# Six neighbouring channels to a partition, and the first image's group statistics by two masked products

## The chip, the cores and the metric

The kernel runs on one core of a Trainium2 chip. The metric is the device time of one launch in microseconds (us); lower is better. Engines are named as in the profile: PE is TensorE (PEld its weight loads), DVE is VectorE, ACT is ScalarE, POOL is GpSimd, and SP is SyncE, which here only issues transfers.

## The reference

Two residual layers run in series over four images of 32 x 32 positions and 768 channels. Each layer normalises its input in 32 groups of 24 neighbouring channels, applies attention with 12 heads of width 64 and decomposed relative positions, projects, and adds the input back.

```python
def _gn(v, G=32, eps=1e-5):
    g = v.reshape(B_, H_, W_, G, C_ // G)
    m = jnp.mean(g, axis=(1, 2, 4), keepdims=True)
    s = jnp.var(g, axis=(1, 2, 4), keepdims=True)
    return ((g - m) / jnp.sqrt(s + eps)).reshape(v.shape)

def attention(x, ...):                      # layer 1 has biases and another position table
    q, k, v = heads(x @ Wqkv)
    bias = rel_h[..., :, None] + rel_w[..., None, :]
    attn = softmax(scale * (q @ k.T) + bias)
    return heads_back(attn @ v) @ Wproj + bproj

x = x + attention_0(_gn(x))
x = x + attention_1(_gn(x))
```

The mean and the variance of a group are taken over all 1024 positions and over its 24 channels.

## The kernel before

The input is held channels first: an image is 768 rows (channels) of 1024 positions, in fp32. A channel chunk `c` (six of them, `NC`) is 128 channels, one to a partition; half `h` of an image is 512 positions. So a tile `xn_0_c_h` is 128 x 512, and partition p of chunk c holds channel 128c + p. All weights are laid out on the host to match, before the timed span.

There are eight image passes (two layers of four images), each of six pairs of heads, each of eight units of 128 query positions. A loop over the 384 units writes out by hand the order of instructions on every engine. `load_x` brings tiles of x, `fetch` the residuals (`res`) and output weights, `put_result` adds a projected part and stores it (`part`, then `mid` between the layers, or `out`).

A unit computes scores (L443), softmax (L455, L459, L473 or L471), transposes the probabilities on DVE (L479), writes them to memory (`td`) and reads them back in another order (`pt`) for the product with v (L508). Beside that the query, key and value products of the next pair (L285, L313) and output projections run. The q, k products use sums and differences of weight quarters and of image tiles: `combine` on POOL makes weight quarters (L129), `sums` on POOL makes image sums s2, s3, s4 (L257).

All of this starts with a normalisation. `stats` takes bn_stats of each half tile (L188) and bn_aggr per channel (L191), which gives mean and variance per channel in `mv` (128 x 6 x 2). The group step, `norm`, has five stages: `gather` writes `mv` to memory as 768 pairs (`per`, L208), `by_group` reads it back with one group to a partition (`g`, 32 x 24 x 2, L211), `groups` combines means and variances (L215 to L218), `inverses` makes scale and shift per channel and writes them to memory (`back`, L225), and `spread` reads them with a channel to a partition (`nrm`, L228). `apply` then scales each tile in place, on ACT (L233) or on DVE (L235).

For image 0 all five stages stand one behind the other, on the ACT queue, before the first product. For the seven later image passes they are spread over the units of pair 3 of the pass before, on the SP queue, with the applies in pair 4:

```python
queue = nc.sync if im else nc.scalar
queue.dma_start(out=per.rearrange("(c p) s -> p c s", p=P), in_=mv_of[im])
...
stages, apply = norm(0)
for n in sorted(stages):
    stages[n]()
for stage in range(2):
    combine(0, stage)
for h in range(2):
    for c in range(NC):
        apply(c, h, c % 2 == 1)
```

The SP queue is one queue for `td`, `pt`, `rel`, `res`, `part`, weights and x, in the order in which the loop issues them. PSUM tiles of tag `m` (two buffers) and the `pt` tiles (two buffers) rotate.

Of the kernel before, what the change touches and what calls it, by code (L numbers as in the profile page):

```python
# [31 lines left out]
FP = mybir.dt.float32  # L32
AF = mybir.ActivationFunctionType
ALU = mybir.AluOpType
ENGINES = {getattr(mybir.EngineType, e) for e in ("PE", "DVE", "Activation", "Pool", "SP")}

P = 128
B, HW, C = 4, 32, 768
S = HW * HW
NH, D = 12, 64  # L40
NC = C // P
NT = S // P
NG, GS = 32, C // 32
EPS = 1e-5
SCALE = D ** -0.5
HALF = 512
LAYERS = 2
NP = NH // 2
# [8 lines left out]
def attention_blocks(ctx: ExitStack, tc: tile.TileContext, a: dict, out: bass.AP):  # L57
    nc = tc.nc
# [12 lines left out]
    ptpool = ctx.enter_context(tc.tile_pool(name="pt", bufs=2))  # L71
# [3 lines left out]
    small = ctx.enter_context(tc.tile_pool(name="small", bufs=4))  # L75
# [4 lines left out]
    ps_m = ctx.enter_context(tc.tile_pool(name="ps_m", bufs=2, space=PSUM))  # L80
# [3 lines left out]
    srcs = [[a["x"][b] for b in range(B)], mid]  # L84
    dsts = [mid, [out[b] for b in range(B)]]
# [4 lines left out]
    xn_of = {im: [[], []] for im in range(NI)}  # L90
    w_of, wv_of, wo_of = {}, {}, {}

    def load_x(im, c, h, half=None):

        l, b = images[im]
        if c == len(xn_of[im][h]):
            xn_of[im][h].append(xpool.tile([P, HALF], FP, tag="xn", name=f"xn_{im}_{c}_{h}"))
        half = h if half is None else half
        nc.sync.dma_start(
            out=xn_of[im][h][c],  # L100
            in_=srcs[l][b][c * P : (c + 1) * P, half * HALF : (half + 1) * HALF],
        )

    def weights_of(g, name):
# [32 lines left out]
    def combine_values(g):  # L137

        w = wv_of[g]
        nc.gpsimd.tensor_tensor(w[:, NB:], w[:, NB:], w[:, :NB], ALU.subtract)  # L140

    for c in range(NC):
        for h in range(2):
            load_x(0, c, h)
# [9 lines left out]
    for l in range(LAYERS):  # L154
        tab = const.tile([P, 2, 2 * HW], FP, tag=f"tab{l}", name=f"tab{l}")
        nc.gpsimd.memset(tab, 0.0)
        for i, ax in enumerate("hw"):
            src = a[f"rel{ax}{l}"]
            n = src.shape[1]
# [10 lines left out]
    for l in range(LAYERS):  # L170
# [7 lines left out]
    mv_of = {  # L178
        im: const.tile([P, NC, 2], FP, tag=f"mv{im}", name=f"mv_{im}") for im in range(NI)
    }  # L180
    half_stats = {}

    def stats(im, c, i, x):

        if im not in half_stats:
            half_stats[im] = small.tile([P, NC, 2, 6], FP, tag="st", bufs=2, name=f"st_{im}"), set()
        st, done = half_stats[im]
        nc.vector.bn_stats(st[:, c, i, :], x)  # L188
        done.add((c, i))
        if (c, 1 - i) in done:  # L190
            nc.vector.bn_aggr(mv_of[im][:, c, :], st[:, c].rearrange("p i s -> p (i s)"))  # L191

    def norm(im):

        per = dram2.tile([C, 2], FP, tag="per", name=f"per_{im}")
        back = dram2.tile([C, 2], FP, tag="back", name=f"back_{im}")  # L200
        g = small.tile([NG, 2, GS, 2], FP, tag="g", bufs=1, name=f"g_{im}")
        st = small.tile([NG, 2, 6], FP, tag="gst", bufs=1, name=f"gst_{im}")
        mv = small.tile([NG, 3, 2], FP, tag="gmv", bufs=1, name=f"gmv_{im}")
        nrm = small.tile([P, NC, 2], FP, tag="nrm", bufs=2, name=f"nrm_{im}")
        queue = nc.sync if im else nc.scalar

        def gather():
            queue.dma_start(out=per.rearrange("(c p) s -> p c s", p=P), in_=mv_of[im])  # L208

        def by_group():  # L210
            queue.dma_start(out=g[:, 0, :, :], in_=per.rearrange("(g k) s -> g k s", k=GS))  # L211

        def groups():
            for k in range(2):
                nc.vector.bn_stats(st[:, k, :], g[:, 0, :, k])  # L215
                nc.vector.bn_aggr(mv[:, k, :], st[:, k, :])
            nc.vector.tensor_scalar(mv[:, 2, 0:1], mv[:, 0, 1:2], mv[:, 1, 0:1], EPS, ALU.add, ALU.add)
            nc.scalar.activation(mv[:, 2, 1:2], mv[:, 2, 0:1], AF.Sqrt)  # L218

        def inverses():  # L220
            nc.vector.reciprocal(mv[:, 2, 0:1], mv[:, 2, 1:2])
            nc.vector.tensor_scalar(mv[:, 2, 1:2], mv[:, 0, 0:1], mv[:, 2, 0:1], -1.0, ALU.mult, ALU.mult)
            for k in range(2):
                nc.vector.tensor_copy(g[:, 1, :, k], mv[:, 2, k : k + 1].to_broadcast([NG, GS]))
            queue.dma_start(out=back.rearrange("(g k) s -> g k s", k=GS), in_=g[:, 1, :, :])  # L225

        def spread():
            queue.dma_start(out=nrm, in_=back.rearrange("(c p) s -> p c s", p=P))  # L228

        def apply(c, h, scalar=True):  # L230
            x = xn_of[im][h][c]
            if scalar:
                nc.scalar.activation(x, x, AF.Identity, bias=nrm[:, c, 1:2], scale=nrm[:, c, 0:1])  # L233
            else:
                nc.vector.tensor_scalar(  # L235
                    x, x, nrm[:, c, 0:1], nrm[:, c, 1:2], ALU.mult, ALU.add
                )

        return {1: gather, 2: by_group, 4: groups, 5: inverses, 7: spread}, apply

    sum_tiles = {}
# [279 lines left out]
    def cuts(im):  # L521
        return [0, NC // 2, NC] if im + 1 < NI else [0, NC // 2, NC - 1, NC]
# [6 lines left out]
    part_of, res_of, sum_of = {}, {}, {}  # L529
    fetched = [0, 0]  # L530

    def fetch(upto):

        while fetched[0] <= min(upto, len(parts) - 1):
            im, p, o, i = parts[fetched[0]]
            c0, c1 = cuts(im)[p : p + 2]
            if i == 0:
                w = wopool.tile([P, NC // 2, P], FP, tag="wo", name=f"wo_{im}_{p}_{o}")
                nc.sync.dma_start(
                    out=w[:, : c1 - c0, :],  # L540
                    in_=a[f"wo{images[im][0]}"][o][:, c0 * P : c1 * P].rearrange(
                        "p (c o) -> p c o", o=P
                    ),
                )
                for c in range(c0, c1):
                    wo_of[im, o, c] = w[:, c - c0, :]
            fetched[0] += 1
        while fetched[1] <= min(upto, len(parts) - 1):
            im, p, o, i = parts[fetched[1]]
            l, b = images[im]  # L550
            if (p, o, i) == (0, 0, 0) and im + 1 < NI:
                part_of[im] = dram2.tile([C, S], FP, tag="part", name=f"part_{im}")
            res = iopool.tile([P, HALF], FP, tag="res", name=f"res_{im}_{p}_{o}_{i}")
            res_of[im, p, o, i] = res
            src = srcs[l][b] if p == 0 else part_of[im]
            nc.sync.dma_start(out=res, in_=src[o * P : (o + 1) * P, i * HALF : (i + 1) * HALF])
            fetched[1] += 1

    def fetch_last():
# [36 lines left out]
    def put_result(im, p, o, i, t):  # L596
        l, b = images[im]
        end = im + 1 == NI
        rows = slice(o * P, (o + 1) * P)
        cols = slice(i * HALF, (i + 1) * HALF)  # L600
        if end and p == 0:
            sum_of[o, i] = xpool.tile([P, HALF], FP, tag="xn", name=f"sum_{o}_{i}")
        to = sum_of[o, i] if end else res_of[im, p, o, i]
        if p == 0:
            res = res_of[im, p, o, i]
            nc.vector.scalar_tensor_tensor(to, t, bo[l][:, o : o + 1], res, ALU.add, ALU.add)
        else:
            nc.vector.tensor_tensor(to, t, to, ALU.add)
        if p == 1 and l + 1 < LAYERS:
            stats(im + B, o, i, to)  # L610
        dst = (part_of[im] if p == 0 and not end else dsts[l][b])[rows, cols]
        if not end:
            early.append(lambda: nc.sync.dma_start(out=dst, in_=to))
        elif p == 2:
            nc.sync.dma_start(out=dst, in_=to)
        if i == 1 and (im, p, o, i) in place:
            if end:
                fetch(place[im, p, o, i] + 4)
            else:
                later.append(lambda: fetch(place[im, p, o, i] + 4))  # L620
# [63 lines left out]
    with tc.manual_schedule(engines=ENGINES):  # L684
        for c in range(NC):
            for i in range(2):
                stats(0, c, i, xn_of[0][i][c])
        stages, apply = norm(0)
        for n in sorted(stages):
            stages[n]()  # L690
        for stage in range(2):
            combine(0, stage)
        for h in range(2):
# [46 lines left out]
        for at, (g, n) in enumerate(units):  # L740
            im, pair = divmod(g, NP)
            end = im + 1 == NI
            if n == 0:
# [7 lines left out]
                if pair == 3 and not end:  # L751
                    stages, apply = norm(im + 1)
# [6 lines left out]
            if (pair, n) in loads and not end:  # L759
                load_x(im + 1, loads[pair, n], 0)  # L760
            if pair == 4 and n in (1, 2) and not end:
                for c in range(3 * n - 3, 3 * n):
                    load_x(im + 1, c, 1)
            if im + 1 < B:
                if pair == 0 and n < NC:
                    load_x(im + 1, n, 0, 1)
                c = n - 2 if pair == 0 else loads.get((pair, n - 2), loads.get((pair - 1, n + 6), -1))
# [44 lines left out]
            if n == 4 and pair % 2 and g + 1 < NPAIR:  # L812
                combine_values(g + 1)
# [76 lines left out]
```

## Time and profile before

| what | value |
|---|---|
| median of 3 runs | 3369.71 us (3365.89 to 3370.19) |
| the profiled execution: its time | 3373.25 us |
| the profiled execution: its span | 3370.8 us |
| PE busy | 3319.2 us, 98% |
| DVE, ACT, POOL busy | 2415.5, 2039.6, 2332.4 us |
| transfers | 1046.97 MB in 534777 packets, mean 311 GB/s |
| transfers under 512 B | 149728 packets |
| first product of image 0 | 26.72 us after the start of the span |

The span is what the profiler saw from the first to the last instruction; the execution's own time is 2.45 us longer. A busy PE is matmuls in flight, whose ends are modelled. Idle time of an engine counts only where it is on the chain that ended last.

### The profile page before, as it was taken

How to read it: one execution, taken by the hardware profiler on the slowest of the kernel's cores; microseconds unless marked ns; L12 is line 12 of the kernel's file. 1: busy time of each engine (PE TensorE's matmuls, PEld its weight loads, DVE VectorE, ACT ScalarE, POOL GpSimd, SP SyncE). 2: the span in 40 equal slices, each digit the busy share in tenths (PEclk: the TensorE clock that was granted, in tenths of full speed). 3: DMA queues.
4: the chain of work that ended last, by engine and by line, in shares of the span. 5: the costliest groups of instructions: out<-in, count | busy, mean ns of one | idle time of the engine just before them, and what ended most of it. 6: DMA issues, size and time to landing. Idle time of an engine off the chain costs nothing.

```text
span 3370.8 us, 58086 instructions
## 1 busy us (share of the span) xinstructions
PE 3319.2 (98%) x21600; PEld 1875.8 (56%) x21600; DVE 2415.5 (72%) x3923; ACT 2039.6 (61%) x3140; POOL 2332.4 (69%) x1184
## 2 busy tenths in 40 slices
PE   6999999999999999999999999999999999999998
PEld 3555555555555555555555555555555555555554
DVE  3787677777777677777777777667776677767775
ACT  2666756566565666566655666566665657665563
POOL 5777866678666686666866668676686667766662
PEclk9999999999999999999999999999999999999999
DMA  3899989899998998889888999989998999898887
GB/s 113 297 330 312 336 306 338 319 306 335 321 322 314 315 331 312 312 300 334 320 309 315 316 321 330 317 306 313 337 313 308 334 306 335 301 324 299 312 290 263
DMA packets 534777, 1046.97 MB, mean 311 GB/s; under 512 B 149728, under 2 KB 212704, under 8 KB 485344
## 3 DMA queue, kind: packets, MB, share of 16 engines
q1 hardware_dynamic: 479936, 1015.84, 85.6%
q10 hardware_dynamic: 54560, 27.43, 2.8%
q8 instruction: 171, 2.80, 0.3%
q14 instruction: 110, 0.90, 0.1%
HBM read 568.01 MB, written 475.10 MB: 309 GB/s over the span
## 4 chain that ended last, share of the span: by engine, by line
PE 93%; DMA 4%; DVE 2%; issue 1%; ACT 0%; SPq 0%; POOL 0%; ACTq 0%; DVEq 0%
PE pj L285 21%; PE av L508 19%; PE s L443 19%; PE pv L285 15%; PE oo L285 13%; PE pj L313 3%; PE tp L381 3%; DMA td<-tb 2%; DMA pt<-td 1%; PE o L587 1%; DVE tb L479 1%; DMA xn<-in_x 0%; DVE sc L455 0%; DVE st L188 0%; DMA per<-mv 0%
## 5 line engine op out<-in xcount | busy, mean ns | idle before, releaser
L429 POOL TENSOR_TENSOR sc<-rel 128x1024 f32<-128x1024 f32 x768 | 1880.3, 2478 | 636.8 <-DVE tb L479 601.6
L455 DVE CUSTOM_DVE_ANT_0 sc<-s,sc 128x1024 f32<-128x1024 f32 x768 | 910.9, 1225 | 524.0 <-PE s L443 459.5
L459 ACT ACTIVATE sc<-sc,sm 128x1024 f32<-128x1024 f32 x768 | 878.5, 1146 | 484.9 <-DVE sm L455 483.8
L473 ACT ACTIVATE sc<-sc,sm 128x1024 f32<-128x1024 f32 x674 | 743.0, 1143 | 580.3 <-DVE sm L467 454.1
L479 DVE STREAM_TRANSPOSE tb<-sc 128x1024 f32<-128x1024 f32 x768 | 909.6, 1226 | 60.9 <-DMA td<-tb 56.8
L443 PE MATMUL s<-k,q 64*128 64x512 f32 x3072 | 738.6, 596 | 2.6 <-DVE sm L455 2.6
L508 PE MATMUL av<-pt,v 128*64 128x256 f32 x6144 | 687.5, 381 | 10.1 <-DMA pt<-td 9.0
L508 PEld LDWEIGHTS av<-pt,v 128*64 128x64 f32 x6144 | 436.2, 137 | 290.6 <-issue 48.5
L285 PE MATMUL pv<-wv,xn 64*128 64x256 f32 x4608 | 523.5, 376 | 1.0 <-DVE wv L274 1.0
L285 PEld LDWEIGHTS pv<-wv,xn 64*128 64x128 f32 x4608 | 447.7, 187 | 114.5 <-issue 55.2
L285 PE MATMUL oo<-attn,wo 64*128 64x512 f32 x2112 | 475.3, 589 | 0.0
L443 PEld LDWEIGHTS s<-k,q 64*128 64x128 f32 x3072 | 289.2, 187 | 316.1 <-issue 292.5
L285 PEld LDWEIGHTS oo<-attn,wo 64*128 64x128 f32 x2112 | 200.9, 187 | 228.0 <-issue 227.1
L471 POOL TENSOR_SCALAR sc<-sc,sm 128x1024 f32<-128x1024 f32 x94 | 105.1, 1118 | 305.7 <-DVE sm L467 295.6
L285 PE MATMUL pj<-xn,wa 64*128 64x512 f32 x1152 | 269.4, 598 | 30.6 <-DVE xn L235 26.7
L285 PE MATMUL pj<-xn,w 64*128 64x512 f32 x1152 | 263.3, 589 | 1.6 <-DVE w L274 1.6
L285 PE MATMUL pj<-s,wc 64*128 64x512 f32 x576 | 262.6, 589 | 0.0
L285 PE MATMUL pj<-s,w 64*128 64x512 f32 x576 | 262.6, 589 | 0.0
L285 PEld LDWEIGHTS pj<-xn,wa 64*128 64x128 f32 x1152 | 113.6, 189 | 166.5 <-issue 126.7
L285 PEld LDWEIGHTS pj<-xn,w 64*128 64x128 f32 x1152 | 111.6, 187 | 137.4 <-issue 134.9
L404 ACT COPY rel<-raw 32x256 f32<-32x256 f32 x384 | 155.1, 404 | 30.6 <-DMA part<-res 10.9
L285 PEld LDWEIGHTS pj<-s,wc 64*128 64x128 f32 x576 | 107.6, 187 | 67.6 <-issue 66.9
(68 smaller groups left out, 2118.5 us busy)
## 6 DMA issues: line engine op xcount, KB each, us to landing
td<-tb SPq DMA_DIRECT2D x384, 1024.0 KB, 6.6
pt<-td SPq DMA_DIRECT2D x382, 1024.0 KB, 9.0
tdr<-t ACTq DMA_DIRECT2D x96, 256.0 KB, 6.5
part<-res SPq DMA_DIRECT2D x84, 256.0 KB, 5.0
res<-part SPq DMA_DIRECT2D x84, 256.0 KB, 4.7
wa<-in_wqk SPq DMA_DIRECT2D x48, 384.0 KB, 3.3
wc<-in_wqk SPq DMA_DIRECT2D x48, 384.0 KB, 6.3
wv<-in_wv SPq DMA_DIRECT2D x24, 768.0 KB, 12.4
```

The source lines that it names most:

```text
L285: nc.tensor.matmul(to, lhsT=w, rhs=x, start=(half, at) == (0, 0), stop=(half, at) == (1, n - 1))
L313: nc.tensor.matmul(t[:, h, :], lhsT=w[rows, c, :], rhs=x[c][rows, :], start=(c == 0), stop=(c == NB - 1),)
L381: nc.tensor.matmul(ps[:, h, j, :], lhsT=q[rows, at * P : (at + 1) * P], rhs=tabs[l][rows, :], start=True, stop=True,)
L404: nc.scalar.copy(rel[rows, :, 0, :, :], raw[rows, :, :, WIDE - 1 - HW - y : WIDE - 1 - y])
L429: nc.gpsimd.tensor_tensor(sc.rearrange("p (a k) (u l) -> p a (k u) l", a=4, l=8), rel[:, h, 0, m, :].unsqueeze(1).unsqueeze(3).to_broadcas ...
L443: nc.tensor.matmul(ps[h][:, cols], lhsT=q[rows, n * P : (n + 1) * P], rhs=k[rows, cols], start=True, stop=True,)
L455: nc.vector.tensor_tensor_reduce(out=sc, in0=ps[h], in1=sc, scale=-scale, scalar=BIG, op0=ALU.add, op1=ALU.min, accum_out=st[:, 0, h : h + 1],
L459: nc.scalar.activation(sc, sc, AF.Exp, bias=st[:, 0, h : h + 1], scale=-1.0, accum_out=st[:, 1, h : h + 1],)
L471: nc.gpsimd.tensor_scalar(sc, sc, st[:, 2, h : h + 1], 1.0, ALU.mult, ALU.mult)
L473: nc.scalar.mul(sc, sc, st[:, 2, h : h + 1])
L479: nc.vector.transpose(tb[:, :, h, :], sc_of[g, n, h])
L508: nc.tensor.matmul(av[rows, at * 2 * P : (at + 1) * 2 * P], lhsT=v_of[g][:, k, rows], rhs=pt_of[g, quarter].rearrange("p n r k h i -> p (n ...
```

## The change

Channels are placed differently: partition p holds channels 6p to 6p + 5, chunk c being channel 6p + c, so that a group of 24 channels is four neighbouring partitions. All transfers of x, `res`, `part`, `mid` and `out` take rows through `chunk`, and the host lays out weights and biases to match.

The first image's group statistics stay on the chip. A mask `same_group` (128 x 128, one where two partitions share a group) is built on POOL in a buffer of the `pt` pool. `norm_first` sums the six channel means in each partition, multiplies by the mask, which leaves the group's sum on all four of its partitions, and does the same for the squared offsets plus variances. Scale and shift are then one number per partition, for all six chunks. The later images keep the way through memory, with `per` and `nrm` now moved in runs of 12 numbers in place of 2.

```diff
+    def chunk(rows, c):
+        return rows.rearrange("(p c) s -> p c s", c=NC)[:, c, :]
...
-            in_=srcs[l][b][c * P : (c + 1) * P, half * HALF : (half + 1) * HALF],
+            in_=chunk(srcs[l][b], c)[:, half * HALF : (half + 1) * HALF],
...
+    same_group = ptpool.tile([P, 2, 4, NT, 2, HW], FP, tag="pt", name="same_group")
+    same_group = same_group.rearrange("p n r k h i -> p (n r k h i)")[:, :P]
+    nc.gpsimd.memset(same_group, 1.0)
+    for sign, base in ((1, 0), (-1, GS // NC - 1)):
+        nc.gpsimd.affine_select(
+            out=same_group, in_=same_group, pattern=[[-sign * (GS // NC), NG], [0, GS // NC]],
+            compare_op=ALU.is_ge, fill=0.0, base=base, channel_multiplier=sign,
+        )
...
+    def norm_first():
+        mv = mv_of[0]
+        w = small.tile([P, 2, NC], FP, tag="nrm", bufs=2, name="nrm_work")
+        nrm = small.tile([P, NC, 2], FP, tag="nrm", bufs=2, name="nrm_0")
+        total = ps_m.tile([P, 2, HALF], FP, tag="m", name="groups_0")[:, :, 0]
+        work = nrm.rearrange("p c s -> p (c s)")
+        part, mean, inv, shift = (work[:, k : k + 1] for k in range(4))
+        off, var = w[:, 0, :], w[:, 1, :]
+        nc.vector.tensor_reduce(part, mv[:, :, 0], mybir.AxisListType.X, ALU.add)
+        nc.tensor.matmul(total[:, 0:1], lhsT=same_group, rhs=part, start=True, stop=True)
+        nc.vector.tensor_scalar(mean, total[:, 0:1], 1.0 / GS, None, ALU.mult)
+        nc.vector.tensor_scalar(off, mv[:, :, 0], mean, None, ALU.subtract)
+        nc.vector.tensor_tensor(var, off, off, ALU.mult)
+        nc.vector.tensor_tensor(var, var, mv[:, :, 1], ALU.add)
+        nc.vector.tensor_reduce(part, var, mybir.AxisListType.X, ALU.add)
+        nc.tensor.matmul(total[:, 1:2], lhsT=same_group, rhs=part, start=True, stop=True)
+        nc.vector.tensor_scalar(inv, total[:, 1:2], 1.0 / GS, EPS, ALU.mult, ALU.add)
+        nc.scalar.activation(part, inv, AF.Sqrt)
+        nc.vector.reciprocal(inv, part)
+        nc.vector.tensor_scalar(shift, mean, inv, -1.0, ALU.mult, ALU.mult)
+
+        def apply(c, h, scalar):
+            x = xn_of[0][h][c]
+            if scalar:
+                nc.scalar.activation(x, x, AF.Identity, bias=shift, scale=inv)
+            else:
+                nc.vector.tensor_scalar(x, x, inv, shift, ALU.mult, ALU.add)
+        return apply
...
-            queue.dma_start(out=per.rearrange("(c p) s -> p c s", p=P), in_=mv_of[im])
+            queue.dma_start(out=per.rearrange("(p c) s -> p c s", c=NC), in_=mv_of[im])
...
-            queue.dma_start(out=nrm, in_=back.rearrange("(c p) s -> p c s", p=P))
+            queue.dma_start(out=nrm, in_=back.rearrange("(p c) s -> p c s", c=NC))
...
-            nc.sync.dma_start(out=res, in_=src[o * P : (o + 1) * P, i * HALF : (i + 1) * HALF])
+            nc.sync.dma_start(out=res, in_=chunk(src, o)[:, i * HALF : (i + 1) * HALF])
...
-        dst = (part_of[im] if p == 0 and not end else dsts[l][b])[rows, cols]
+        dst = chunk(part_of[im] if p == 0 and not end else dsts[l][b], o)[:, cols]
...
-        stages, apply = norm(0)
-        for n in sorted(stages):
-            stages[n]()
+        apply = norm_first()
...
-        w = w.reshape(NC, P, 3, NP, P)[:, :, :2]
-        return w.transpose(3, 2, 1, 0, 4).reshape(NP, 2, P, NC * P)
+        w = w.reshape(P, NC, 3, NP, P)[:, :, :2]
+        return w.transpose(3, 2, 0, 1, 4).reshape(NP, 2, P, NC * P)
...
-        return w.reshape(NC, P, NC, P).transpose(2, 1, 0, 3).reshape(NC, P, NC * P)
+        return w.reshape(NC, P, P, NC).transpose(3, 1, 0, 2).reshape(NC, P, NC * P)
...
-        "bo0": np.asarray(L0_conv_bproj).reshape(NC, P).T,
+        "bo0": np.asarray(L0_conv_bproj).reshape(P, NC),
```

The order of instructions stays as it is on every engine apart from these: on PE the two products stand ahead of all others; on DVE nine instructions are exchanged for nine; ACT issues four transfers fewer; on POOL the mask's three instructions come first, with the memsets of the two position tables between them, and the copies and scaling of the second table move behind the first image sum.

More of the change, by code (lines that the diff above doesn't have):

```diff
@@ L204, in norm @@
         nrm = small.tile([P, NC, 2], FP, tag="nrm", bufs=2, name=f"nrm_{im}")
-        queue = nc.sync if im else nc.scalar
+        queue = nc.sync
         def gather():
-            queue.dma_start(out=per.rearrange("(c p) s -> p c s", p=P), in_=mv_of[im])
+            queue.dma_start(out=per.rearrange("(p c) s -> p c s", c=NC), in_=mv_of[im])
         def by_group():
@@ L227, in spread, with apply @@
         def spread():
-            queue.dma_start(out=nrm, in_=back.rearrange("(c p) s -> p c s", p=P))
-        def apply(c, h, scalar=True):
+            queue.dma_start(out=nrm, in_=back.rearrange("(p c) s -> p c s", c=NC))
+        def apply(c, h):
             x = xn_of[im][h][c]
[L232 to L237, printed above, removed]
+            nc.scalar.activation(x, x, AF.Identity, bias=nrm[:, c, 1:2], scale=nrm[:, c, 0:1])
         return {1: gather, 2: by_group, 4: groups, 5: inverses, 7: spread}, apply
@@ L598, in put_result @@
         end = im + 1 == NI
-        rows = slice(o * P, (o + 1) * P)
         cols = slice(i * HALF, (i + 1) * HALF)
@@ L846, in by_pair @@
     def by_pair(w):
-        w = w.reshape(NC, P, 3, NP, P)[:, :, :2]
-        return w.transpose(3, 2, 1, 0, 4).reshape(NP, 2, P, NC * P)
+        w = w.reshape(P, NC, 3, NP, P)[:, :, :2]
+        return w.transpose(3, 2, 0, 1, 4).reshape(NP, 2, P, NC * P)
     def by_two(w):
-        w = w[:, 2 * C :].reshape(NC, P, NP // 2, 2 * P)
-        return w.transpose(2, 1, 0, 3).reshape(NP // 2, P, NC * 2 * P)
+        w = w[:, 2 * C :].reshape(P, NC, NP // 2, 2 * P)
+        return w.transpose(2, 0, 1, 3).reshape(NP // 2, P, NC * 2 * P)
     def by_output(w):
-        return w.reshape(NC, P, NC, P).transpose(2, 1, 0, 3).reshape(NC, P, NC * P)
+        return w.reshape(NC, P, P, NC).transpose(3, 1, 0, 2).reshape(NC, P, NC * P)
     def table(r):
@@ L872 @@
         "bqkv1": np.asarray(L1_conv_qkv_b).reshape(3 * NP, P).T,
-        "bo0": np.asarray(L0_conv_bproj).reshape(NC, P).T,
-        "bo1": np.asarray(L1_conv_proj_b).reshape(NC, P).T,
+        "bo0": np.asarray(L0_conv_bproj).reshape(P, NC),
+        "bo1": np.asarray(L1_conv_proj_b).reshape(P, NC),
         "relh0": table(L0_conv_rel_pos_h),
```

## The prediction

> **What bounds the kernel now.** I read the page first: the busy shares (its part 1) and the chain that ended last (part 4).
>
> ```profile
> span 3370.8 us, 58086 instructions
> PE 3319.2 (98%) x21600; PEld 1875.8 (56%) x21600; DVE 2415.5 (72%) x3923; ACT 2039.6 (61%) x3140; POOL 2332.4 (69%) x1184
> PE 93%; DMA 4%; DVE 2%; issue 1%; ACT 0%; SPq 0%; POOL 0%; ACTq 0%; DVEq 0%
> ```
>
> PE is the bound: 3319.2 of 3370.8 us busy, which leaves 51.6 us in which something else can be gained. The waits, filtered to PE, say where those lie (us in total, times, longest):
>
> ```profile
> PE pj L285 <- DVE xn L235: 26.7, 1, 26.7
> PE av L508 <- DMA pt<-td: 9.0, 6, 2.6
> ```
>
> More than half is one wait: nothing can be multiplied before image 0 is normalised. The chain of waits of the first 70 us shows what fills it (start, duration):
>
> ```profile
> 13.73 0.22 DVE mv L191
> 13.97 4.72 DMA per<-mv
> 18.76 2.18 DMA g<-per
> ...
> 22.74 1.34 DMA back<-g
> 24.10 1.99 DMA nrm<-back
> 26.12 0.56 DVE xn L235
> 26.72 5.60 PE pj L285 x10
> ```
>
> Channel statistics are ready at 13.95; four small transfers in series take 4.72 + 2.18 + 1.34 + 1.99 = 10.2 us of the 12.2 us up to 26.12. Then the table of stretches, for the slack later on (PE, PEld, DVE, ACT, POOL busy, clock, DMA share, GB/s):
>
> ```profile
> 446.10:514.80 68.70, 68.70 (x454) 38.90 (x452) 51.27 (x82) 39.62 (x63) 44.33 (x22) 1.00 0.92 325
> 1124.00:1193.00 69.00, 67.95 (x448) 38.59 (x446) 47.45 (x77) 44.88 (x69) 46.53 (x23) 1.00 0.92 330
> ```
>
> A pair of heads takes 68.7 us and PE fills it wholly; DMA, at 0.92, is next. The second stretch is one of the few later ones with a PE gap (1.05 us), just after an image's group gather.
>
> **What the Trainium skill says.** "SBUF — State Buffer", section "Who interferes with whom": VectorE and GpSimd share a port pair under an exclusive lock; a VectorE instruction in a two-port mode (tensor_scalar can be), or with two SBUF inputs against a GpSimd read, blocks until the other ends, or blocks it. The trace agrees for tensor_scalar: L235 takes 540 ns, but 1499 ns for the one that meets a POOL sum at 28.12. For tensor_tensor with two SBUF inputs no row of before tells. "DMA: Bandwidth & Descriptors", section "Specifications": transfers want runs of 512 B or more for line rate. The trace agrees: per<-mv, 6 KB in 768 runs of 8 B, lands after 8.5 us (median on SP), res<-part, 256 KB in 2 KB runs, after 4.7. Same page, "Latency and other measured facts": row pitches of megabytes cost bandwidth, 512 KiB hardly; 24 KiB is not measured there, nor by this trace. "TensorE: Matmul & The Clock Gate", section "What's actually happening": TensorE starts at half clock until some microseconds of work have passed. The trace agrees in durations (64x512 products: 1.06 us at 32.12, 0.59 at 35.28), so this ramp only moves along with the start.
>
> **The change part by part.** All times are within the profiled execution, which took 3373.25 us (span 3370.8), 3.5 above the median of the runs, 3369.71; I subtract from the median.
>
> *Removed:* image 0's gather, by_group, back and spread (four ACT-queue transfers), nine DVE instructions and the table load's late start. The load has nothing ahead of it on ACT any more: 1.28 us, hidden under the x loads.
>
> *Added, on the path from 13.97:* reduce 0.15 (L274 reduces of 128x1); product; tensor_scalar from PSUM 0.20 (L217); three DVE instructions on 128x6, 0.20 each; reduce 0.15; product; tensor_scalar 0.20; Sqrt 0.20 (L218); reciprocal 0.15; tensor_scalar 0.20 (L222). These are 0.15 + 0.20 + 0.60 + 0.15 + 0.20 + 0.20 + 0.15 + 0.20 = 1.85 us. A 128x128 by 128x1 fp32 product is in no row. From below: the weight load alone, 0.19 warm (L587). From above: two cold loads at 0.33 (one at 31.15) and a whole cold narrow product, about 1.0. I take 0.75, twice 1.5. Eleven handovers at 0.03 (as 21.85 to 21.89, L217 to Sqrt) are 0.35. Sum 3.7: applies could start at 17.7 in place of 26.12, a gain of 8.4.
>
> *Added, against it: the lock.* In that interval POOL works back to back on the weight combinations:
>
> ```profile
> 14.95 0.99 POOL L129 TENSOR_TENSOR w<-wc,wa 128x384 f32<-128x384 f32 x1 [13.89 <-DMA wc<-in_wqk]
> 16.02 0.99 POOL L129 TENSOR_TENSOR wc<-wc 128x384 f32<-128x384 f32 x1
> 16.97 0.99 POOL L129 TENSOR_TENSOR w<-wc,w 128x384 f32<-128x384 f32 x1
> 18.04 0.99 POOL L129 TENSOR_TENSOR w<-wa,w 128x384 f32<-128x384 f32 x1
> ```
>
> Before, DVE was idle then. Now the subtract (possibly two-port), the two tensor_tensors on 128x6 and the shift may each wait for the rest of a POOL instruction: at least nothing; at most some 2.6 us, if subtract waits to 15.94, square to 17.0, add to 18.1, and shift to 19.9 behind the table scaling L166. I take 1.1: applies at 18.8, gain 7.3. The applies themselves (0.54 on DVE, 0.80 mean on ACT) may meet the last combination; PE takes 5.3 us cold over its first six products and needs the third DVE tile only 2.5 us in, so that wait is mostly covered.
>
> *At nothing:* the mask (memset, two affine_selects on 128x128) heads POOL at 0.7 us. The nearest POOL row of this shape is L166, 0.53, so about 1.3; it would have to exceed 13 us to reach the first product, and POOL waits for wc until 14.95 anyway. The second table's copies and scaling (0.36 + 0.53) now stand behind the first image sum and delay the others by 0.9; on the times of before PE needs the s2 sums at 44.5 and POOL has the last at 39.6, so 4.9 us cover it. wv lands at 16.7, before PE's new need at about 25. The mask's buffer and the PSUM slot rotate out before their next users. Bias, weight and output orders change only in memory outside the timed span; their transfers keep their shape.
>
> *Does the rest move along?* From 26.72 everything is released by PE, POOL or transfers issued after PE's work; DMA share between 16 and 40 us is under 0.3, so no transfer stands at a fixed time. I count the whole 7.3.
>
> *Moved in memory:* later images' per and nrm transfers go from 768 runs of 8 B to 128 of 48 B, seven times. They stand in the SP queue ahead of td and pt, for which PE waits. All stretches after a gather are full but two: gaps of 1.05 at 1125 and 0.49 at 1537. From below nothing, from above 1.5; I take 0.9. The groups between, and SP's order, are the same.
>
> The x, res, part, mid and out transfers keep 128 runs of 2 KB, at a pitch of 24 KB instead of 4. There are 474 of them (part 6 and the list of issues), 60,672 packets, 124 of 1047 MB. I take no change of rate: pitch is the only thing that differs. Below nothing: if at the start the loads ran at the weights' 418 GB/s rather than 258 (2 to 4 us), the statistics would end up to 1 us earlier (VectorE waits 0.95 at 6.56). Above nothing: the slower rival.
>
> **Sum:** 7.3 + 0.9 = 8.2; 3369.7 - 8.2 = 3361.5. What PE waits for next at the start is VectorE and ScalarE's statistics chain itself, then the x loads.
>
> **The rivals.**
>
> *Full lock (not told from no change).* Every small DVE instruction loses to a combination: applies at 20.3, gain 5.8, nothing from the gathers: 3363.9. For it: POOL has no gap over 0.1 us there. Against: the mean and the reduces read PSUM or one input, and one of the four is a single element wide.
>
> *No lock, faster loads.* Applies at 17.7 or earlier, gathers' 1.5: 3369.7 - 8.4 - 1.5 = 3359.8, with up to 1 us more from the loads. For it: the reciprocals L467 (one input) keep to 109 to 253 ns beside a busy POOL.
>
> *Slower: the 24 KB pitch.* If rows so far apart collide in memory, each 2 KB packet takes longer. One takes 96 to 118 ns now (311 packets in 93.5% of 16 engines' 2 us; 280 in 103.1%). 474 transfers over 48 pairs are 1264 packets a pair, 0.107 x 1264 / 16 = 8.5 us; the DMA share of 0.90 to 0.93 leaves some 5.9 us a pair. It decides from about 70% longer packets; at twice the time each of 47 pairs loses 2.6 us: 3361.5 + 122 = 3484, and somewhat less than 70% already shows in bursts. For it: the x loads at the start reach only 258 GB/s at full DMA share, where weights, in runs of 3 and 6 KB, reach 418 (12 to 14 us), so x packets are sensitive to something. Against: no power of two, and pitches much larger are harmless by the page.
>
> **How the numbers follow.** Middle case 0.42 (own range 3360 to 3363), full lock 0.22, no lock 0.24, pitch 0.12. A measurement of this kernel tells 0.2% (6.7 us) from no change, so the line is 3363.0: faster 0.42 + 0.24 = 0.66, within 0.22, slower 0.12. The range 3355 to 3367 takes in the first three with the runs' own spread (4.3 us over three) and leaves out the pitch case and about 0.06 of tails.
>
> **What would show it.** No per, g, back or nrm transfer before 100 us; first product of 128x1 near 14.2, second near 17; first apply between 17.7 and 20.3; first pj within 0.7 of it. Lock: 128x6 instructions of 0.2 us starting when a POOL row ends. Pitch: res, part and xn landing times against 4.7, 5.0 and 6.6, and DMA share in steady pairs against 0.92. Later gathers: per and nrm landing well under 8.5 and 10.1. I am wrong if the first pj comes before 18 or after 21, or if pairs after 250 us stop filling PE.

## The result, and the profile after

The changed kernel takes 3358.69 us (median of 7 runs, 3355.25 to 3360.76) against 3369.71 (7 runs, 3365.89 to 3373.98). The ratio is 0.9969, with a 95% interval of 0.9957 to 0.9981: faster by 11.0 us by the medians, by 6.4 to 14.5 by the interval. 3361.5 was predicted.

The profiled execution of the changed kernel took 3358.64 us. Its page, busy shares and chain:

```profile
span 3356.7 us, 58091 instructions
PE 3316.0 (99%) x21604; PEld 1874.7 (56%) x21604; DVE 2417.8 (72%) x3923; ACT 2041.0 (61%) x3140; POOL 2333.9 (70%) x1187
PE 95%; DMA 3%; DVE 1%; issue 0%; ACT 0%; SPq 0%; POOL 0%; ACTq 0%; DVEq 0%
```

PE idles 40.7 us in place of 51.6 and is still the bound. The waits of PE in the changed kernel (us in total, times, longest):

```profile
PE groups L216 <- DVE nrm L215: 15.0, 1, 15.0
PE av L547 <- DMA pt<-td: 5.5, 5, 1.7
...
PE groups L222 <- DVE nrm L221: 2.4, 1, 2.4
...
PE pj L324 <- DVE xn L233: 1.5, 1, 1.5
```

Both lines shown of before have shrunk. The wait of 26.7 us at the start is now 15.0 + 2.4 + 1.5 = 18.9, with two short products between; the waits for `pt` went from 9.0 to 5.5. The chain of waits of the changed kernel (start, duration) shows what stands where four transfers stood:

```profile
14.49 0.22 DVE mv L204
14.73 0.17 DVE nrm L215
15.04 0.57 PE groups L216 x2
...
15.83 0.81 DVE nrm_work L218
...
16.86 0.86 DVE nrm_work L220
...
17.95 0.60 PE groups L222 x2
...
19.20 0.22 DVE nrm L226
19.45 0.56 DVE xn L233
20.05 4.80 PE pj L324 x10
```

From the end of the statistics to the first apply it is 14.71 to 19.45, 4.7 us, where it was 12.2. The table of stretches of the changed kernel has the two stretches that answer to those of before (PE, PEld, DVE, ACT, POOL busy, clock, DMA share, GB/s):

```profile
440.00:509.00 69.00, 69.00 (x456) 38.97 (x454) 52.03 (x86) 41.13 (x65) 44.31 (x22) 1.00 0.90 320
1115.00:1184.00 69.00, 69.00 (x456) 39.10 (x454) 49.04 (x79) 45.55 (x70) 46.55 (x23) 1.00 0.90 312
```

The stretch after a gather, which had 1.05 us of idle PE, is full. For a comparison of the whole, the span can be cut in four, by the starts of the long run of value products in one early pair (82.91 before, 73.82 after), at the 42 steady pairs' begin (330.56, 321.07) and at their end (3219.72, 3207.37):

| part of the span | before | after | difference |
|---|---|---|---|
| start, up to the second pair | 82.91 | 73.82 | -9.09 |
| rest of the first image | 247.65 | 247.25 | -0.40 |
| 42 steady pairs | 2889.16 | 2886.30 | -2.86 |
| last pairs | 151.08 | 149.33 | -1.75 |
| span | 3370.8 | 3356.7 | -14.1 |

This compares one execution with one; the one of before lay 3.5 us above its median. What is a cause and what is chance had to come from the experiments.

### The profile page after: what moved, and what is told of

Same layout as the page of the kernel before. It is cut to its first block, busy times and chain, and to the rows that moved or that the text cites. A ratio compares the mean times of both kernels' runs of the same rounds, so it can differ in the third digit from the quotient of the medians.

```text
span 3356.7 us, 58091 instructions
## 1 busy us (share of the span) xinstructions
PE 3316.0 (99%) x21604; PEld 1874.7 (56%) x21604; DVE 2417.8 (72%) x3923; ACT 2041.0 (61%) x3140; POOL 2333.9 (70%) x1187
## 4 chain that ended last, share of the span: by engine, by line
PE 95%; DMA 3%; DVE 1%; issue 0%; ACT 0%; SPq 0%; POOL 0%; ACTq 0%; DVEq 0%
PE pj L324 21%; PE av L547 19%; PE s L482 19%; PE pv L324 15%; PE oo L324 13%; PE pj L352 3%; PE tp L420 3%; DMA td<-tb 2%; PE o L626 1%; DMA xn<-in_x 1%; DVE tb L518 1%; DMA pt<-td 1%; DVE st L201 0%; DVE sc L494 0%; POOL sc L468 0%
```

## The experiments

Theory at the outset: the products' shorter chain gives most of the gain and the later gathers a little. Rivals: the gathers give most of it; the lock (VectorE waiting for POOL, as the prediction describes it) eats the chain's gain; placement does something else by its rows 24 KB apart. Below, `pj` and `pv` are the query, key and value products, and a gather is the write of `per`. Each ratio below is to the kernel before on the same chip, with its 95% interval; its distance from 1, times 3371 us (the median of before was 3371.27 to 3372.01 in all four groups), is the gain in us.

**Placement alone.** Image 0 goes through memory again, in runs of 48 B; the mask is still built, and not used.

```diff
-        queue = nc.sync
+        queue = nc.sync if im else nc.scalar
...
-        apply = norm_first()
+        stages, apply = norm(0)
+        for n in sorted(stages):
+            stages[n]()
```

> The new placement alone: image 0's group step goes through memory again, on the ACT queue, in runs of 48 B. Theory (the gain is the products at the start, and what the shorter per and nrm transfers give): first pj between 23.5 and 25.5 us, because per and nrm lose some 1.5 to 3 us against before (26.72); no PE gap near 1120 and 1530; median 3365 to 3368. Rival (the pitch or the runs bring most of it): first pj as late as 25 to 26.7, yet median at 3361 or lower. x loads: if pitch helps or hurts them, the end of the statistics moves from 13.95 as it did in the changed kernel (14.7).

Measured: 3364.35 us, ratio 0.9976 (0.9968 to 0.9985), a gain of 8.1 us (5.1 to 10.8). The first pj starts at 25.17 in place of 26.72, so only 1.6 of that lies at the start. By subtraction some 6.5 us come later: far above my 0.9, and against the pitch rival, which needed a loss.

**The products alone.** The changed kernel, with `per` and `nrm` of later images moved as 768 runs of 8 B again, since the tiles are padded.

```diff
-        im: const.tile([P, NC, 2], FP, tag=f"mv{im}", name=f"mv_{im}") for im in range(NI)
+        im: const.tile([P, NC, 4], FP, tag=f"mv{im}", name=f"mv_{im}")[:, :, :2] for im in range(NI)
...
-        nrm = small.tile([P, NC, 2], FP, tag="nrm", bufs=2, name=f"nrm_{im}")
+        nrm = small.tile([P, NC, 4], FP, tag="nrm4", bufs=2, name=f"nrm_{im}")[:, :, :2]
```

> The changed kernel with mv and nrm of the later images padded, so that per and nrm move in 768 runs of 8 B again. Theory (short runs delay td and pt for which PE waits): per landing back from 4.4 to about 8.5 us, nrm unchanged near 10, gaps of PE of about 1 us after the gathers near 1120 and 1530, median up by 1 to 2 us to 3360 to 3361. Rival (the gaps before were chance in the phase of the queues): per lands at 8.5 but PE stays full there, median within 0.7 us of 3358.7.

Measured: 3364.92 us, ratio 0.9983 (0.9977 to 0.9990), a gain of 5.7 us (3.4 to 7.8), with the first pj at 19.49. This is the start's share without the gathers', at the new pitch. By the ratio the changed kernel has 10.4 or, run again below, 13.1; the gathers thus bring 4.7 to 7.4. These are differences of two medians, each uncertain by 2 us or more.

**The lock.** The quarter `wc`, for which POOL's combinations wait, is loaded behind `wv`, so that POOL starts later.

```diff
-    for name in "ac":
-        load_w(0, name)
+    load_w(0, "a")
...
+    load_w(0, "c")
```

> The changed kernel with the load of wv issued ahead of that of wc, so that POOL's weight combinations begin about 2 us later, after the small DVE instructions. Theory (lock of the port pair): the subtract and the second tensor_tensor on 128x6, 0.80 and 0.84 us in the changed kernel, fall to about 0.2 each, the second product comes at about 16.7 in place of 17.95 and the first pj about 1.2 us earlier; then applies may wait for POOL instead, 0.3 to 1 us. Median 3357 to 3358.5. Rival (those rows are slow of themselves): 0.80 and 0.84 stay and the first pj stays at 20.05.

VectorE's timeline in the changed kernel (start, duration), then POOL's:

```profile
15.83 0.80 DVE L218 TENSOR_SCALAR nrm_work<-mv,nrm 128x6 f32<-128x6 f32 x1
16.66 0.17 DVE L219 TENSOR_TENSOR nrm_work<-nrm_work 128x6 f32<-128x6 f32 x1
16.86 0.84 DVE L220 TENSOR_TENSOR nrm_work<-nrm_work,mv 128x6 f32<-128x6 f32 x1
```

```profile
15.61 0.99 POOL L133 TENSOR_TENSOR w<-wc,wa 128x384 f32<-128x384 f32 x1 [13.29 <-DMA wc<-in_wqk]
16.68 1.00 POOL L133 TENSOR_TENSOR wc<-wc 128x384 f32<-128x384 f32 x1
```

VectorE's timeline in this experiment, with POOL not yet at work:

```profile
15.45 0.23 DVE L218 TENSOR_SCALAR nrm_work<-mv,nrm 128x6 f32<-128x6 f32 x1
15.72 0.17 DVE L219 TENSOR_TENSOR nrm_work<-nrm_work 128x6 f32<-128x6 f32 x1
15.92 0.17 DVE L220 TENSOR_TENSOR nrm_work<-nrm_work,mv 128x6 f32<-128x6 f32 x1
```

In the changed kernel L218 ends at 16.63 and L220 at 17.70, just after the POOL rows that end at 16.60 and 17.68; L219 starts at 16.66, just ahead of the second row, and is not held up. Without POOL they take 0.23 and 0.17. The lock costs 0.57 + 0.67 = 1.24 us. The first pj came at 18.50 (0.37 of the 1.55 us because the statistics ended earlier), and yet the time was 3359.35, ratio 0.9961 (0.9948 to 0.9973): not told from the changed kernel.

**The clock at the start.** In the trace after, the first ten pieces of pj took 4.80 us against 5.60. Sixteen throw-away products of the mask stand before, between and behind the two group products.

```diff
+        def busy(x, n):
+            for _ in range(n):
+                nc.tensor.matmul(idle[:, :P], lhsT=same_group, rhs=x[:, :P], start=True, stop=True)
...
+        busy(same_group, 4)
...
+        busy(same_group, 3)
```

> The changed kernel with 16 throw-away products of the mask (into a PSUM tile that nobody reads) on PE before, between and after the two products of the group statistics. Theory (the first pj and pv products run at half clock because PE was idle, and the two small products shortened that ramp in the changed kernel): the first six pj products end about 2.8 us after their start in place of 4.6, bounded by the applies; first pj at most 0.5 us later; median 3356.5 to 3358. Rival (the ramp depends on the phase of a free-running window and not on work before): the products still take 4.3 to 5.3 us and the median stays at 3358 to 3359.5.

Measured: 3355.84 us, ratio 0.9953 (0.9939 to 0.9967). The table of stretches of this kernel, two of its rows:

```profile
16.00:18.00 2.00, 0.90 (x9) 0.71 (x8) 1.51 (x4) 0.00 (x0) 1.92 (x3) 1.00 0.10 16
22.00:24.00 2.00, 2.00 (x6) 0.83 (x4) 0.94 (x1) 1.31 (x2) 1.82 (x5) 0.50 0.00 0
```

The granted clock was full at 16 to 18 us and half from 20 to 26: the first pj, at 19.76, met it while it was low. The first twelve pieces of pj took 6.26 us, where the changed kernel's took 5.24: in this execution the products ahead did not shorten the slow stretch. (In the tables of the changed kernel and of the one before, the clock column reads 1.00 over their first pj, though its pieces take the same 1.06 us; for the slow stretch at the start, go by durations.) Nor do the two group products ahead make it surely shorter: of the kernels that have them, e9_per8_later takes 5.60 us over those ten pieces, e2_runs8 5.42 and e6_per8 4.53. The three without them (the kernel before, e1_place, e10_before_later) all take 5.60, so whether they help at times stays open. The ratio overlaps the changed kernel's.

**Which gather.** In one group: the changed kernel itself, `per` alone in runs of 8 B (only the `mv` line of the edit of e2_runs8), and `nrm` alone (only its other line).

> The changed kernel itself, beside the kernels of this group on one chip. With the placement alone at -6.9 us and 8 B runs back at -6.4 us against before on their chip, the sum of parts (start about 6.5 earlier than before, gathers about 5) says 11 to 13 us faster than before, ratio 0.9962 to 0.9968. Rival (the parts overlap, one covers the other): ratio 0.9975, no faster than either part.

> The changed kernel with only mv of the later images padded, so that per alone moves in 768 runs of 8 B. Theory (per is what delays td: it stood at 8.8 us to landing with 8 B runs and at 4.4 with 48 B, while nrm took 9.9 either way): most of the loss of the kernel with both in 8 B runs, 4 to 6 us slower than the changed kernel beside it, pair periods of 69 to 72 us in some gathers' pairs. Rival (nrm does it): within 1 us of the changed kernel.

> The changed kernel with only nrm of the later images padded, so that nrm alone moves in 768 runs of 8 B. Theory (per does it): within 1.5 us of the changed kernel beside it, no pair longer than 69.5 us. Rival (nrm does it, by its 768 packets ahead of td, though its own landing time is no longer): 4 to 6 us slower. If both are 2 to 3 us slower, each has a part.

| kernel | median us | ratio | 95% interval |
|---|---|---|---|
| changed kernel | 3357.6 | 0.9961 | 0.9949 to 0.9974 |
| `per` in 8 B | 3365.65 | 0.9985 | 0.9978 to 0.9991 |
| `nrm` in 8 B | 3358.03 | 0.9962 | 0.9949 to 0.9974 |

As far as the intervals tell, all of it is `per`: 8 us by the medians, with intervals apart. The traces place it in the 42 steady pairs. Undisturbed, these take 2886.3 us. In the eight traces with `per` in 48 B they take 2886.3 to 2887.7; with 8 B it is 2889.2 in the kernel before, 2892.0 in e2_runs8 and 2897.3 here.

Two things could pass the delay on. One is SP's own waiting. First in the kernel before, then in the changed one, then with `per` in 8 B:

```profile
SPq L211 <- DMA per<-mv: 8.1, 6, 3.7
```

```profile
SPq L255 <- DMA per<-mv: 0.6, 1, 0.6
```

```profile
SPq L255 <- DMA per<-mv: 14.7, 6, 4.6
```

L211, now L255, is `by_group`, which reads `per` back one stage after `gather` wrote it. The list of issues gives the time from issue to landing (the last column, median), for the changed kernel and then for `per` in 8 B:

```profile
per<-mv SPq DMA_DIRECT2D x7, 6.0 KB, 4.4
...
nrm<-back SPq DMA_DIRECT2D x7, 6.0 KB, 9.8
```

```profile
per<-mv SPq DMA_DIRECT2D x7, 6.0 KB, 9.2
...
nrm<-back SPq DMA_DIRECT2D x7, 6.0 KB, 9.7
```

A `per` of 9.2 us has not landed when SP comes to `by_group`. SP is in order, so the `td` and `pt` behind it wait too, and PE waits for `pt` (7.2 us in six waits in this kernel, 5.5 in five after).

The other is the `td` that SP issues 0.6 us behind `per`, before it comes to `by_group`. Over the seven gathers it lands after 7.8 to 13.8 us with `per` in 8 B (7.3 to 10.8 in the kernel before), and after 5.0 to 7.2 in the changed kernel. The chain of waits of `per` in 8 B goes through this `td` at three of the gathers, and at none through SP's wait for `per`. The last of the three (L252 issues `per`):

```profile
2737.18 0.53 SPq L252
...
2737.80 13.40 DMA td<-tb
...
2752.47 1.20 DVE tb L518
...
2753.70 11.40 DMA td<-tb
...
2766.42 9.28 DMA pt<-td
```

So in these traces the short runs hold up the next transfer of their own queue before SP waits for them.

**A shorter start.** `wc` behind `wv`, and both group sums (means, and variance plus squared mean) ahead of one pair of products.

```diff
+        nc.vector.tensor_reduce(parts[:, 0:1], mv[:, :, 0], mybir.AxisListType.X, ALU.add)
+        nc.vector.tensor_tensor(square, mv[:, :, 0], mv[:, :, 0], ALU.mult)
+        nc.vector.tensor_tensor(square, square, mv[:, :, 1], ALU.add)
+        nc.vector.tensor_reduce(parts[:, 1:2], square, mybir.AxisListType.X, ALU.add)
+        nc.tensor.matmul(total[:, 0:1], lhsT=same_group, rhs=parts[:, 0:1], start=True, stop=True)
+        nc.tensor.matmul(total[:, 1:2], lhsT=same_group, rhs=parts[:, 1:2], start=True, stop=True)
...
+        nc.vector.scalar_tensor_tensor(root, mean, mean, second, ALU.mult, ALU.subtract)
+        nc.scalar.activation(root, root, AF.Sqrt, scale=-1.0)
```

> The changed kernel with two edits at the start: the load of wc behind that of wv, so that POOL's combinations begin after the small DVE instructions, and both group sums (means, and variances plus squared means) in one go, so that PE is asked once. From the rows of the changed kernel and of the one with wc behind: reduce 0.16, square and add 0.17 each, reduce 0.16, product and wait about 0.8, two scalings and a difference 0.16 to 0.2 each, Sqrt, reciprocal, shift as before, 0.03 to 0.04 between: applies about 2.9 us after the first reduce, in place of 4.7; first pj 17.8 to 18.3 against 20.05. Theory (the whole shift carries over): 1.5 to 2.5 us faster than the changed kernel beside it. Rival (what stands behind, the applies against POOL's combinations or the image sums, takes it back): first pj early, but the tp products after them no earlier, and the same time within 1 us.

From its chain of waits:

```profile
13.59 0.22 DVE mv L204
...
14.14 0.56 PE groups L219 x2
14.70 0.44 PE groups L220 x2
...
16.30 0.56 DVE xn L233
...
16.90 4.59 PE pj L324 x10
53.58 3.10 DMA tdr<-t
```

The chain is 2.5 us (13.81 to 16.30) in place of 4.7, and the first pj at 16.90 is 2.0 ahead of the changed kernel in the same group (18.91). But the time was 3358.8, ratio 0.9959 (0.9945 to 0.9972), against 0.9961. At the second pair 1.1 of the 2.0 us were left (72.44 against 73.53), at the steady pairs' begin none (321.52 against 317.25). The first image's stretch from the second pair to the steady ones varies by more than the gain: 243.7 us (e5_after) to 249.1 (this kernel), with 247.25 in the first profile after. The clock has a part in it. Two rows of the table of stretches, first of this kernel, then of the changed one in the same group (clock third from the end):

```profile
61.00:68.00 7.00, 5.47 (x14) 2.39 (x16) 4.89 (x8) 5.67 (x9) 1.50 (x1) 0.52 0.59 196
174.00:177.00 3.00, 3.00 (x16) 2.10 (x17) 0.71 (x1) 0.79 (x2) 0.09 (x1) 0.50 0.99 418
```

```profile
61.00:68.00 7.00, 4.24 (x13) 1.71 (x11) 3.06 (x7) 6.75 (x10) 0.00 (x0) 0.76 0.81 245
174.00:177.00 3.00, 3.00 (x26) 1.67 (x24) 2.67 (x5) 1.98 (x4) 2.44 (x2) 1.00 1.01 407
```

This execution was granted half the clock for 6.8 us near 61 and for 3.4 near 174; the changed kernel's had 3.4 us of it near 65 and none later. That is up to 5.1 us of work lost, by my estimate, against 1.7. The five runs of this kernel also go with the mean clock that they were granted: 3358.8 and 3360.97 us at 0.998, 3355.68 and 3359.33 at 0.999, 3351.62 at 1.000. So the clock can take up the 2 us; whether nothing else does is not settled by one execution of each.

**Is it SP's waiting?** If so, a later `by_group` should cure a slow `per`. Three kernels in one group: `per` in 8 B, the kernel before, and the changed kernel, each with

```diff
-        return {1: gather, 2: by_group, 4: groups, 5: inverses, 7: spread}, apply
+        return {1: gather, 3: by_group, 4: groups, 5: inverses, 7: spread}, apply
```

> The kernel with per alone in 8 B runs, and the reading back of it (by_group) issued one unit, some 8.6 us, later on the SP queue. Theory (the loss is SP standing still until per has landed, 14.7 us in six gathers, with td and pt behind it): the wait of by_group for per falls below 2 us, pairs near a gather last 68.7 to 69.3 us, median 3358 to 3360. Rival (768 packets take the transfer engines' time ahead of td): per still lands after 9 us and the median stays at 3364 to 3366, whatever SP waits.

> The kernel before, old placement and all, with by_group issued one unit later for the later images. Theory (same as above): 4 to 6 us faster than before, ratio 0.9982 to 0.9988, since its start stays as it is; SP's 8.1 us of waiting for per gone. Rival (packets, or the placement itself): within 1.5 us of before. A third outcome: the groups stage on VectorE waits for g instead and nothing is won.

> The changed kernel with by_group one unit later: a control for what the later reading costs of itself. Where per lands in 4.4 us SP waited 0.6 us in all, so nothing is there to win: within 1.5 us of the changed kernel (3357.6 to 3358.7); slower by 1 us a gather if VectorE's groups stage has to wait for g.

| with `by_group` a stage later | median us | ratio | 95% interval |
|---|---|---|---|
| `per` in 8 B | 3400.89 | 1.0083 | 1.0069 to 1.0097 |
| kernel before | 3395.55 | 1.0078 | 1.0066 to 1.0091 |
| changed kernel | 3360.66 | 0.9974 | 0.9964 to 0.9984 |

The first two are 26 us and more slower than the kernel before, by the ratio; set against the same kernels with `by_group` at its old place, that is 26 us for the second and 33 for the first. VectorE's waits, of the first of them and then of the third:

```profile
DVE gst L259 <- DMA g<-per: 27.0, 7, 5.1
```

```profile
DVE gst L259 <- DMA g<-per: 2.5, 3, 1.9
```

`g` takes as long to land in both (10.6 and 9.9 us by the median), but with 8 B it starts later. SP no longer waits for `per` at all; the `td` right behind `per` still lands late (7.5 to 12.7 us over the seven gathers, 4.8 to 7.7 in the third kernel), and a `pt` that needs it stands ahead of `g` in the queue. The chain of the first kernel at one gather (L529 issues `pt`):

```profile
2351.79 0.53 SPq L252
...
2352.42 12.67 DMA td<-tb
...
2365.10 0.37 SPq L529
...
2365.52 10.68 DMA g<-per
...
2378.57 5.49 PE pj L324 x12
```

So `g` lands when `groups`, one stage behind, is already due. VectorE stands, with the next pair's `k` and the softmax behind it in order; the waits of PE in the first kernel show it:

```profile
PE pj L324 <- DVE k L368: 25.1, 7, 4.9
```

So the wait was not removed but moved to a worse engine. The clock adds to it: those twelve pieces of pj take 5.49 us, where 2.58 is usual, since half the clock was granted for 3.4 or 6.8 us behind six of the seven gathers (0.50 from 2378 to 2384 us, for one; 30.7 us in all, so up to 15 us lost by my estimate), where the third kernel's table reads 1.00. With PE's 25.1 us of waiting for `k` that is about the 40 us between the two. The third kernel shows that with runs of 48 B the same order costs little (0.9974 against 0.9961 or 0.9969, intervals overlapping). My expectation, that a later `by_group` would cure a slow `per`, was wrong; that the loss stays with SP's wait gone speaks for the `td` behind `per` rather than for SP's waiting.

**The other end.** `per` in 8 B, with `gather` a stage earlier.

```diff
-        return {1: gather, 2: by_group, 4: groups, 5: inverses, 7: spread}, apply
+        return {0: gather, 2: by_group, 4: groups, 5: inverses, 7: spread}, apply
```

> The kernel with per alone in 8 B runs, and its gather issued one unit earlier, by_group left where it is, so that per has some 8.6 us more to land before SP comes to by_group; the same packets, and VectorE's groups stage not moved. Theory (the loss is SP standing still for per, with td and pt behind it): the wait for per falls from 14.7 us to below 1, pairs near a gather last 68.7 to 69.3, and the time returns to that of the changed kernel, ratio to before 0.9959 to 0.9969. Rival (the 768 packets delay td by themselves): the wait is gone all the same, but the ratio stays at 0.998 to 0.999. Between the two: each has a part.

Measured: 3361.28 us, ratio 0.9969 (0.9958 to 0.9980), though `per` now takes 12.4 us to land. SP's waits have one line left for it, at another place (L454 loads the position tables' products, `rel`):

```profile
SPq L454 <- DMA per<-mv: 3.7, 3, 2.6
```

About 5 of the 8 us come back (0.9985 to 0.9969, whose intervals overlap by a hair; 3365.65 to 3361.28), with the same 768 packets. This doesn't tell the two ways apart, for both were eased: SP waits less, and at the six later gathers the next `td` is issued 4.2 to 5.1 us behind `per` in place of 0.6 and lands after 9.5 to 10.2 us. Its steady pairs take 2889.9 us, 2 to 4 more than with 48 B. Whether the other 2.7 us (0.9969 to 0.9961) are what is left of them or nothing stays open, since those intervals overlap widely.

What is shown, then, is that the run length of `per` costs the 8 us and that giving `per` more time takes back about half. How it is split between the delayed `td` and SP's waiting is argued from the chains of single executions, which speak for the `td`.

No kernel was measurably faster than the changed one: e3_wc_last, e4_warm and e8_best lie at 0.9953 to 0.9961, inside the interval of its second measurement (0.9949 to 0.9974).

## Why the prediction was right, and where its sum was wrong

**The chain at the start: right.** I summed 3.7 us, plus 1.1 for the lock, and 4.7 was measured. The group products took 0.57 and 0.60 where I took 0.75; the lock took 1.24 where I took 1.1. By the 7.3 the first pj was to come at 19.4; it came at 20.05 here, because the statistics ended at 14.71 in place of 13.95, and at 18.91 in the second profile of the same kernel, where they ended at 13.47. They follow the loads of x, and so move by over a microsecond from one execution to the next.

**"I count the whole 7.3": somewhat too much, perhaps.** The kernel that changes the start and keeps the 8 B runs gains 5.7 (3.4 to 7.8), the one with `per` alone in 8 B 5.1 (3.0 to 7.4). The interval admits 7.3, but e8_best gained 2.0 more at the first pj and nothing in the end. I considered only transfers at a fixed time; the first image's pairs and the granted clock can take up a microsecond or two. Of the 9.09 us in the table above, the slow stretch at the start (0.8) and `tdr` landing after 2.31 us in place of 3.20 (0.9) vary by execution: e9_per8_later took 5.60 us over the ten pieces, as the kernel before did, and e8_best had 3.10 for `tdr`.

**The later gathers: the mis-sized term.** I took 0.9, and 1.5 from above; the runs show 4.7 to 7.4 by e2_runs8, 8 by e6_per8. The mechanism was the one I named (in the SP queue ahead of `td` and `pt`), but I sized it by idle PE in two stretches of one execution, 1.05 + 0.49. Other readings of that same trace would have said more. The `td` right behind `per` landed after up to 10.8 us, where 6.6 is the median of all. SP's waits had a line of 8.1 us for `per` at L211. And the pairs' periods, 68.72 us each, had four long ones (70.19, 69.11, 69.55, 68.89) that add to 2.9 us, though the idle PE I counted was 1.5. The ends of busy products are modelled, which may hide the rest; the period hides nothing. Even 2.9 is less than the medians show: how the waits fall differs by execution (the steady pairs of e6_per8's profile lost 11.0, in one pair of 74.26 us half of it, with 3.4 us of half clock behind the wait). Where the rest of the loss of the kernel before lies, its one trace doesn't show.

So by the medians 7.3 was some 2 too high and 0.9 some 5 too low. That they partly cancelled was luck, and is why 3361.5 was only 2.8 us off.

**Full lock: no.** L226, one element wide, took 0.21 us at 19.20 in the middle of a POOL row (18.72 to 19.71), as did L217, which reads PSUM, beside the first: 0.16. **No lock: no**, but e3_wc_last shows that its absence would not have been seen in the time.

**The 24 KB pitch: no.** `res` landed in 4.8 us, `part` in 4.2 and `xn` from the input in 6.6, where it was 4.7, 5.0 and 6.9 before; the DMA share of a steady pair is 0.90. **At nothing: right for the mask**, done by 2.3 us (memset 0.20, two affine_selects 0.53 and 0.52).

## What to carry to other kernels

Price a small transfer by what stands behind it in its queue, not by its bytes: read when the next transfers of that queue land, the waits of the issuing queue itself, and the periods of the steady loop, before sizing a stall by the bound engine's idle time. A reader moved a stage later passed the wait on to VectorE and made two kernels 26 and 33 us slower; longer runs, or the producer issued earlier, were the moves that helped here. Microseconds won at the first product are not yet won at the end, while a stage that isn't yet steady lies between.

## What the runs showed of the hardware

- A VectorE instruction with two SBUF inputs does wait for a POOL tensor_tensor: 128x6 took 0.84 us beside it, 0.17 without. The Trainium skill's "SBUF — State Buffer", section "Who interferes with whom", says so; the prediction had no row of before to test it by.
- On the busy SP queue, 768 runs of 8 B took a write to memory twice as long to land as 128 runs of 48 B (`per`, 9.2 against 4.4 us), while a read showed no difference (`nrm`, 9.6 against 9.8). On the ACT queue at the start it was 4.7 against 3.5 and 2.0 against 1.7 (kernel before, e1_place). The Trainium skill's "DMA: Bandwidth & Descriptors", section "Specifications", speaks of runs under 512 B without that difference.
- A transfer issued 0.6 us behind such a write on the same queue lands late too: `td` after 7.8 to 13.8 us behind runs of 8 B, 5.0 to 7.2 behind runs of 48 B.
- Some products ahead did not keep TensorE's clock up: after sixteen of them it was granted at 0.50 from 20 to 26 us. Behind PE's waits of up to 4.9 us in e9_per8_later it was granted at 0.50 too, for 3.4 or 6.8 us. The ten pieces of pj at the start took 4.53 to 5.60 us, by execution.
